# Graph attention over sorted edges: the reverse scan of maxima in halves, its marks in PSUM, q's products in two banks

## The chip, the cores and the metric

The kernel runs on one core of a Trainium2 chip. The metric is the device time of one execution in microseconds (us); the median of several runs counts. The engines are PE (TensorE), DVE (VectorE), ACT (ScalarE), POOL (GpSimd) and SP (SyncE, which here issues DMAs). PE writes its results to PSUM, eight banks of 512 fp32 columns for each of the 128 partitions; everything else lies in SBUF or in HBM. POOL has no access to PSUM in this kernel and does nothing in the stage of interest but issue gathers (indirect DMAs) and write zeros.

## The reference

A graph network layer on 6250 nodes of 128 features and 200,000 edges sorted by their target `dst`: two convolutions over the edges, then an attention of 8 heads with 16 columns each. The change touches the attention alone:

```python
q = (h @ qw + qb).reshape(n, H, HD)
k = (h @ kw + kb).reshape(n, H, HD)
v = (h @ vw + vb).reshape(n, H, HD)
logits = (q[dst] * k[src]).sum(-1) * scale + (edge_attr @ ew + eb)
amax = jax.ops.segment_max(logits, dst, num_segments=n)
pe = jnp.exp(logits - amax[dst])
ssum = jax.ops.segment_sum(pe, dst, num_segments=n)
w = pe / jnp.clip(ssum[dst], 1e-06)
o = jax.ops.segment_sum(w[:, :, None] * v[src], dst, num_segments=n)
```

All of it is fp32.

## The kernel before

The edges are cut into 196 chunks of 1024 (`CH`), each of eight tiles of 128 (`NT`). Since `dst` is sorted, a chunk's targets lie in a window of 112 nodes, so q of the targets is fetched by a product with a one-hot matrix, and sums over targets are products with another one. k and v of the sources are fetched from HBM by gathers: eight per chunk, each 128 rows of 256 fp32 numbers, issued by POOL at L621, followed by four memsets (L633) as a pause. A gathered chunk `g` has one of eleven buffers (L1155), which is free again when the chunk's `v` has been made (L1236).

The attention works in runs: eight chunks make a run, and the last three runs have six, four and two. `pipeline` (L712) is a loop over iterations n; in iteration n it

- starts loads and gathers of chunk n+1 (`fetch`), and prepares its one-hot `ohT` on ACT (`compared`, L614 and L615, in place);
- calls `second`: if a run ended with chunk n-1, its maxima are made (`maxima`, L1197), in pieces between other work; and one chunk of the run before, some nine chunks back, is finished: the comparison `oh` (L638), the addition of the chunk before it to the tables (L1262 to L1268), the weighted values `v` (ACT at L1235, L1337 and L1338, DVE at L1236), the sums `u` on PE (L1243), and the merging of the chunk before (L1250 to L1258, L1276, L1279);
- calls `first` for chunk n: `logits` (L1174) multiplies the gathered k by q (L1179, in three pieces of three, three and two tiles), copies the edges' bias out of PSUM (ACT, L1180), reduces by heads (L1182) and adds (L1184);
- moves a batch of finished nodes one step on (`attention_nodes`, L863; a batch of four windows starts every eight iterations from iteration 44 on, and uses DVE at L867 to L895 and L786 to L788);
- makes q's products of chunk n+1 on PE (`products`, L1163): `ohT` times the rows `pk`, eight tiles into three PSUM tiles `qe` of one bank each (L1166, three buffers), so that they are ready one iteration ahead.

DVE, ACT, PE and SP each keep the order in which the program issues (`in_order`, L700); POOL's gathers follow their buffers. fp32 products take two passes on PE per tile of 128 edges: 16 passes for a chunk's `u`, 16 for its `qe`.

`maxima` gives every edge the maximum of its segment within the run, for up to 64 rows (8 chunks times 8 heads) of 1024 edges. The logits are transposed in two halves of 512 (`lt`, PSUM, L1208); a forward scan over each half (L1211) takes the running maximum, and adds -1e30 where a segment begins (marks `nbs`). One reverse scan over all 1024 (L1214) then carries each segment's last value back, with the marks `nbe` of where segments end. Both marks are bf16 in SBUF, `fw` is fp32 in SBUF. Eight transposes (L1218) bring the result back as `rm`; L1222 subtracts it from the logits, ACT takes the exponential `pe` (L1224), and L1226 picks the maxima at the segments' ends (`wl`).

In PSUM the stage has `iota`, three banks of `qe`, `blk` (shared by `lt`, `rm` and the nodes' products), `pe` and two of `u`: all eight banks.

Of the kernel before, what the change touches and what calls it, by code (L numbers as in the profile page):

```python
# [8 lines left out]
FP = mybir.dt.float32  # L9
# [3 lines left out]
ALU = mybir.AluOpType  # L13
# [8 lines left out]
P = 128  # L22
D = 128
H = 8
HD = 16
NT = 8
CH = NT * P
REST = 4
G = 8
# [5 lines left out]
KW = WN + KE  # L35
DB = D + H
# [4 lines left out]
BIG = 1e30  # L41
# [4 lines left out]
def kernel(ctx: ExitStack, tc: tile.TileContext, x, src, dst, eat, w, out):  # L46
# [9 lines left out]
    nc = tc.nc  # L56
    N = x.shape[0]
    EW = src.shape[1]
    NCH = EW // NT
# [74 lines left out]
    a_d = {i: dram.tile([(NW + 1) * P, D], FP, name=f"a_d{i}") for i in (1, 2, 3)}  # L134
# [549 lines left out]
    def left_rows(k, pools, rows_d, tag, shape, bufs):  # L684

        lp = pools["left"]
        k.rows = lp.tile([P, DB], FP, name="l_rows")
        nc.vector.memset(k.rows[:, D:], 0.0)
        nc.sync.dma_start(out=k.rows[:, :D], in_=rows_d[bass.ds(k.win * P, P), :])
        onehot(k, pools, iota_j)  # L690
        k.ohf = lp.tile([P, NT, P], FP, name="l_ohf")
        per = shape[1]
        for a in range(0, NT, per):
            n = min(per, NT - a)
            tp = pools["ps"].tile(shape, FP, name="l_tp", tag=tag, bufs=bufs)
            for t in range(n):
                nc.tensor.transpose(tp[:, t, :P], k.oh[:, a + t, :], ident)
            nc.scalar.copy(k.ohf[:, a:a + n, :], tp[:, :n, :P])
# [453 lines left out]
    with ExitStack() as es:  # L1152
        pool = lambda n, b, **kw: es.enter_context(tc.tile_pool(name=f"{n}a", bufs=b, **kw))
        pools = {"oh": pool("oh", 2), "ps": pool("ps", 1, space=PSUM)}
        gp, wk, vp = pool("gp", G + 3), pool("wk", 2), pool("vp", 1)  # L1155
        ps_ = pools["ps"]
# [4 lines left out]
        TB = 3  # L1161

        def products(k, terms):  # L1163

            for a in range(0, NT, TB):
                qe = ps_.tile([P, TB, DB], FP, name="qe", tag="qe", bufs=3)  # L1166
                for t in range(min(TB, NT - a)):
                    e = slice((a + t) * P, (a + t + 1) * P)
                    for j, (lhs, rhs) in enumerate(terms):
                        nc.tensor.matmul(qe[:, t, :], lhsT=lhs[:, e], rhs=rhs,  # L1170
                                         start=(j == 0), stop=(j == len(terms) - 1))
                k.qe.append(qe)

        def logits(k, lg):  # L1174
            ebs = wk.tile([P, NT, H], FP, name="ebs")
            for a, qe in zip(range(0, NT, TB), k.qe):
                n = min(TB, NT - a)
                kk = k.g[:, a:a + n, :D]
                nc.vector.tensor_tensor(kk, qe[:, :n, :D], kk, ALU.mult)  # L1179
                nc.scalar.copy(ebs[:, a:a + n, :], qe[:, :n, D:])  # L1180
            l3 = wk.tile([P, NT, H], FP, name="l3")
            nc.vector.tensor_reduce(  # L1182
                l3, k.g[:, :, :D].rearrange("p t (h c) -> p t h c", c=HD), AX.X, ALU.add)
            nc.vector.tensor_tensor(lg, l3, ebs, ALU.add)  # L1184
# [12 lines left out]
        def maxima(run, lg, nb, bp):  # L1197

            n, c0 = len(run), run[0].c
            q = n * H
            fw = bp.tile([G * H, CH], FP, name="fw")
            half = CH // 2
            for a in range(2):
                lt = ps_.tile([G * H, 4, P], FP, name="lt", tag="blk")
                for t in range(4):
                    nc.tensor.transpose(lt[:q, t, :], lg[:, 4 * a + t, :n, :].rearrange("p c h -> p (c h)"), ident)  # L1208
                yield
                at = slice(a * half, (a + 1) * half)  # L1210
                nc.vector.tensor_tensor_scan(  # L1211
                    fw[:q, at], nb["nbs"][:q, at], lt[:q].rearrange("p t e -> p (t e)"),
                    fw[:q, half - 1:half] if a else -BIG, ALU.add, ALU.max)
            nc.vector.tensor_tensor_scan(  # L1214
                fw[:q, ::-1], nb["nbe"][:q, ::-1], fw[:q, ::-1], -BIG, ALU.add, ALU.max)
            rm = ps_.tile([P, NT, G, H], FP, name="rm", tag="blk")
            for t in range(NT):
                nc.tensor.transpose(rm[:, t, :n, :].rearrange("p c h -> p (c h)"), fw[:q, t * P:(t + 1) * P], ident[:q, :q])  # L1218
            yield
            wl = vp.tile([P, NT, G, H], FP, name="wl")  # L1220
            e3 = ef[:, c0 * NT:(c0 + n) * NT].rearrange("p (c t) -> p t c", t=NT)
            nc.vector.tensor_tensor(lg[:, :, :n, :], lg[:, :, :n, :], rm[:, :, :n, :], ALU.subtract)  # L1222
            pe = ps_.tile([P, NT, G, H], FP, name="pe", tag="pe")
            nc.scalar.activation(pe[:, :, :n, :], lg[:, :, :n, :], AF.Exp)  # L1224
            for t in range(NT):
                nc.vector.tensor_tensor(  # L1226
                    wl[:, t, :n, :], rm[:, t, :n, :], e3[:, t, :, None].to_broadcast([P, n, H]), ALU.mult)
            for j, k in enumerate(run):
                k.pe, k.wl = pe[:, :, j, :], wl[:, :, j, :]
# [56 lines left out]

        class Stage:
            sums, late, nb = [], [], None
            lg, j = None, 0

            def __init__(self, bp):
                self.bp = bp
# [8 lines left out]
                return k  # L1301

            def products(self, k):
                products(k, [(k.ohT[:KW], k.pk[:KW])])

            def first(self, k):
                if self.j == 0:
# [2 lines left out]
                self.j += 1  # L1310

            def reduce(self, k):
                pass

            def root(self, run):
                if self.nb is None and self.runs:
# [2 lines left out]
            def second(self, run, ks):  # L1319


                pieces = iter(())
                if run:
                    pieces = maxima(run, self.lg, self.nb, self.bp)
                    self.nb, self.j = None, 0
                for n, k in enumerate(ks):
                    mine = pieces if n == len(ks) - 1 else iter(())
                    next(mine, None)
                    onehot(k, pools, iota)
                    next(mine, None)  # L1330


                    if self.late:
                        add_late(self.late.pop(0))
                    next(mine, None)
                    weighted(k)
                    nc.scalar.copy(k.v[:, :, VK:VK + H], k.wl)  # L1337
                    nc.scalar.copy(k.v[:, :, VK + H], ef[:, k.c * NT:(k.c + 1) * NT])  # L1338
                    sums(k, VK + H + 1)
                    if self.sums:  # L1340
                        merge_late(self.sums[0])
                        self.late.append(self.sums.pop())
                    self.sums.append(k)
                for _ in pieces:
                    pass

            def batch(self, j):
                w = nc.values_load(at_i[3][0:1, j:j + 1], engines=[DVE, SP], min_val=0,
# [15 lines left out]

        def left(k):
            lp = pools["left"]
            left_rows(k, pools, a_d[3], "qe", [P, TB, DB], 3)
            k.g = gp.tile([P, NT, KV], FP, name="g")
            gather(k, k.g, kv_d, pause=False)
            k.qe = []  # L1370
            products(k, [(k.ohf.rearrange("p t e -> p (t e)"), k.rows), (k.ea, webl)])
            lg = lp.tile([P, NT, H], FP, name="l_lg")
            logits(k, lg)
            neg = lp.tile([P, 4, P], FP, name="l_neg")
            part = lp.tile([P, H, 2], FP, name="l_part")
            junk = lp.tile([P, 4, P], FP, name="l_junk")
            for a in range(2):
                nc.vector.tensor_scalar(neg, k.ohf[:, 4 * a:4 * a + 4, :], 1.0, BIG, ALU.subtract, ALU.mult)
                for h in range(H):
                    bc = ps_.tile([P, 4, P], FP, name="l_bc", tag="blk")  # L1380
                    for t in range(4):
                        nc.tensor.transpose(bc[:, t, :], lg[:, 4 * a + t, h:h + 1].to_broadcast([P, P]), ident)
                    nc.vector.tensor_tensor_reduce(
                        junk, bc, neg, 1.0, -BIG, ALU.add, ALU.max, part[:, h, a:a + 1])
            cm = lp.tile([P, H], FP, name="l_cm")
            nc.vector.tensor_reduce(cm, part, AX.X, ALU.max)
            me = ps_.tile([P, NT, H], FP, name="l_me", tag="pe")
            for t in range(NT):
                nc.tensor.matmul(me[:, t, :], lhsT=k.ohf[:, t, :], rhs=cm, start=True, stop=True)
            nc.vector.tensor_tensor(lg, lg, me, ALU.subtract)  # L1390

            nc.vector.tensor_scalar(lg, lg, 0.0, None, ALU.min)
            k.pe = lp.tile([P, NT, H], FP, name="l_pe")
            nc.scalar.activation(k.pe, lg, AF.Exp)
            weighted(k)
            sums(k, VK)
            tt = t3[:, bass.ds(k.win, 1), :]
            merge(k, M[:, bass.ds(k.win, 1), :], None, cm[:, None, :], 1)
            add(k, tt, 1)
# [43 lines left out]
```

## Time and profile before

| what | us |
|---|---|
| median of 3 runs | 7322.78 (7318.51 to 7324.84) |
| profiled execution | 7334.91 |
| its span | 7333.2 |
| first gather of the attention starts | 4865.6 |
| last one ends | 7255.3 |

| 4860 to 7260 us | busy us of 2400 | instructions |
|---|---|---|
| POOL | 1876.05 | 2352 |
| DVE | 1693.49 | 3755 |
| PE | 1322.40 | 6815 |
| PE weight loads | 1230.38 | 6813 |
| ACT | 732.95 | 2045 |

The DMA engines were busy 51% of this stretch, at 139 GB/s, and PE's granted clock was 0.72 of full speed.

How to read the profile's lines: a group has its source line, engine and operation, what it writes and reads (`out<-in`), the shape, the count, then the busy time in us and the mean duration in ns, then how long the engine was idle just before these instructions and what ended that. "issue" is idle time that ended with nothing the profile shows. A line of the waits has the waiting instruction, what ended the wait, and the total in us, the number and the longest. A line of the timeline has the start and the duration in us; neighbours of the same kind are merged, with their count. A reader should keep in mind that an engine's share of busy time does not tell whether it sets the pace; who waits for whom does.

### The profile page before, as it was taken

The page shows a single profiled execution, that of the slowest core. Times are in us where ns is not written, and L with a number is a line of the kernel's source. Part 1 is how long each engine was busy: PE and PEld are TensorE (multiplying, and loading weights), DVE is VectorE, ACT ScalarE, POOL GpSimd, SP SyncE. Part 2 cuts the span into 40 slices and gives each one's busy share as a digit, 9 for nine tenths or more (in the row PEclk, how much of TensorE's full clock was granted, in tenths as well). Part 3 has the DMA queues.
Part 4 walks back from the last instruction along what each step waited for, and adds up shares of the span by engine and source line. Part 5 has one row for each costly group of instructions (what it writes and reads, how often), then busy time and mean ns, then how long its engine had stood idle before and what let it go on. Part 6 is the DMA issues. An engine that isn't in the chain of part 4 may idle for free. (4 is left out here: it accounts for less than half of the span.)

```text
span 7333.2 us, 74261 instructions
## 1 busy us (share of the span) xinstructions
PE 3791.1 (52%) x20957; PEld 3613.5 (49%) x20958; DVE 5146.2 (70%) x7564; ACT 3312.2 (45%) x5293; POOL 5573.4 (76%) x7070
## 2 busy tenths in 40 slices
PE   4445454445554454455455555545555555555554
PEld 4444444445544444454454554444545555555554
DVE  6766677677777566666777777746667777777777
ACT  5555555555555455555555555532223333333332
POOL 6777777777777577777777777767777777777774
PEclk7777777777777667767777777767777777777777
DMA  5433333333333333333333333345445555555553
GB/s 144 108 94 92 85 106 89 97 94 94 98 96 92 77 88 89 91 90 87 97 99 101 97 100 103 99 102 137 135 135 142 141 138 145 143 142 138 140 139 86
DMA packets 414323, 800.46 MB, mean 109 GB/s; under 512 B 101813, under 2 KB 274984, under 8 KB 379496
## 3 DMA queue, kind: packets, MB, share of 16 engines
q0 software_dynamic: 175616, 411.34, 21.5%
q1 hardware_dynamic: 232646, 380.69, 19.1%
q10 hardware_dynamic: 5632, 3.51, 0.2%
q8 instruction: 172, 2.82, 0.2%
q14 instruction: 257, 2.11, 0.1%
HBM read 754.19 MB, written 40.96 MB: 108 GB/s over the span
## 5 line engine op out<-in xcount | busy, mean ns | idle before, releaser
L621 POOL DMA_INDIRECT g<-b_d,src_i x3136 | 3004.4, 958 | 979.9 <-issue 958.0
L1023 PE MATMUL u<-h,oh 128*128 128x129 f32 (+1 forms) x6272 | 1352.3, 402 | 2290.3 <-ACT h L1018 1952.6
L1023 PEld LDWEIGHTS u<-h,oh 128*128 128x128 f32 x6272 | 1248.2, 304 | 2365.9 <-ACT h L1018 2005.9
L621 POOL DMA_INDIRECT g<-kv_d,src_i x1568 | 1539.8, 982 | 502.1 <-issue 471.7
L999 DVE TENSOR_TENSOR h<-m,g 128x1024 f32<-128x1024 f32 x392 | 479.3, 1223 | 1055.6 <-DMA g<-b_d,src_i 939.4
L1243 PE MATMUL u<-v,oh 128*128 128x145 f32 x3136 | 754.0, 427 | 767.2 <-DVE nm L1276 553.2
L1243 PEld LDWEIGHTS u<-v,oh 128*128 128x128 f32 x3136 | 702.0, 310 | 801.9 <-issue 801.9
L633 POOL MEMSET nst<- 128x392 f32 x2352 | 1011.3, 430 | 101.7
L993 PE MATMUL m<-pk,ohT 117*128 117x128 f32 x6272 | 926.7, 311 | 29.1 <-ACT ohT L615 24.9
L993 PEld LDWEIGHTS m<-pk,ohT 117*128 117x128 f32 x6272 | 917.0, 232 | 30.9 <-ACT ohT L615 25.2
L1018 ACT ACTIVATE h<-h 128x1024 f32<-128x1024 f32 x392 | 414.1, 1056 | 1118.2 <-DVE h L1017 693.3
L1001 ACT ACTIVATE sq<-h 128x1024 f32<-128x1024 f32 x392 | 414.0, 1056 | 933.7 <-DVE h L999 657.8
L1002 DVE TENSOR_REDUCE var<-sq 128x64 f32<-128x1024 f32 x392 | 477.7, 1219 | 296.7 <-ACT sq L1001 240.2
L1179 DVE TENSOR_TENSOR g<-qe,g 128x384 f32<-128x384 f32 (+1 forms) x588 | 294.1, 511 | 554.4 <-DMA g<-kv_d,src_i 450.0
L614 ACT ACTIVATE ohT<-ohT,minus_p 112x1024 f32<-112x1024 f32 x588 | 670.3, 1140 | 14.9 <-DMA ohT<-rel_d 14.6
L615 ACT ACTIVATE ohT<-ohT 112x1024 f32<-112x1024 f32 x588 | 621.2, 1057 | 18.6
L1170 PE MATMUL qe<-pk,ohT 117*128 117x136 f32 x3136 | 515.8, 320 | 158.0 <-ACT ebs L1180 106.5
L1170 PEld LDWEIGHTS qe<-pk,ohT 117*128 117x128 f32 x3136 | 477.7, 226 | 192.1 <-ACT ebs L1180 130.8
L1016 DVE TENSOR_TENSOR h<-h,cps 128x1024 f32<-128x1024 f32 x392 | 478.4, 1220 | 13.5
L1017 DVE TENSOR_TENSOR h<-h,cps 128x1024 f32<-128x1024 f32 x392 | 478.4, 1220 | 13.4
L1013 DVE TENSOR_TENSOR h<-h,cps 128x1024 f32<-128x1024 f32 x392 | 475.3, 1213 | 5.9
L638 DVE TENSOR_TENSOR oh<-cps,dm 128x1024 f32<-128x1024 f32 x392 | 476.0, 1214 | 0.0
(265 smaller groups left out, 4380.3 us busy)
## 6 DMA issues: line engine op xcount, KB each, us to landing
ohT<-rel_d SPq DMA_DIRECT2D x294, 896.0 KB
g<-b_d,src_i POOLq DMA_INDIRECT x3136
pk<-a_d SPq DMA_DIRECT2D x588, 56.0 KB
g<-kv_d,src_i POOLq DMA_INDIRECT x1568
ohT<-in_eat_dram SPq DMA_DIRECT2D x294, 40.0 KB
a_d<-n_o SPq DMA_DIRECT2D x28, 256.0 KB
kv_d<-n_o SPq DMA_DIRECT2D x28, 256.0 KB
n_h<-h_d SPq DMA_DIRECT2D x19, 256.0 KB
```

Of the source, the lines that this page charges most:

```text
L614: nc.scalar.activation(k.ohT[:WN, :], k.ohT[:WN, :], AF.Square, bias=minus_p[:WN])
L615: nc.scalar.activation(k.ohT[:WN, :], k.ohT[:WN, :], AF.Relu, bias=1.0, scale=-4.0)
L621: return nc.gpsimd.indirect_dma_start(out=g[:, t, :table_d.shape[1]], out_offset=None, in_=table_d, in_offset=bass.IndirectOffsetOnAxis(ap ...
L633: last = nc.gpsimd.memset(nst2, 0.0)
L993: nc.tensor.matmul(k.m[:, t, :], lhsT=lhs[:, t * P:(t + 1) * P], rhs=rhs, start=(j == 0), stop=(j == len(terms) - 1))
L999: nc.vector.tensor_tensor(k.mt, k.m, k.g, ALU.add)
L1002: return lambda: nc.vector.tensor_reduce(var[:, j * NT * H:(j + 1) * NT * H], sq.rearrange("p t (g c) -> p (t g) c", c=HD), AX.X, ALU.add)
L1016: nc.vector.tensor_tensor(k.mt, k.mt, over_edges(gam), ALU.mult)
L1017: nc.vector.tensor_tensor(k.mt, k.mt, over_edges(bet), ALU.add)
L1023: nc.tensor.matmul(k.u[:, :wide], lhsT=k.oh[:, t, :], rhs=k.h[:, t, :wide], start=(t == 0), stop=(t == NT - 1))
L1170: nc.tensor.matmul(qe[:, t, :], lhsT=lhs[:, e], rhs=rhs, start=(j == 0), stop=(j == len(terms) - 1))
L1243: nc.tensor.matmul(k.u[:, :wide], lhsT=k.oh[:, t, :], rhs=k.v[:, t, :wide], start=(t == 0), stop=(t == NT - 1))
```

## The change

Three things are changed, all in the attention:

1. The reverse scan is made in two halves of 512, the later half first, and the earlier half starts from the first value of the later one. The marks of the segments' ends are copied beforehand from SBUF to a PSUM tile `ends` (fp32, one bank, one buffer) by ACT, half by half; the second copy is issued after the first half scan, whose tile it takes over.
2. `qe` has two banks in place of three, which makes the bank for `ends` free. A chunk's third piece of q's products (two tiles) is issued within `logits`, after the first piece has been multiplied and copied out; the first two pieces are issued one iteration ahead as before.
3. The order of the last parts of `maxima` moves: after the first half of the reverse scan comes the weighting, summing and merging of an earlier chunk; the second half and the transposes `rm` come after that; and L1222 to L1226 (subtraction, exponential, maxima at the ends) come after `first`, in `reduce`, except at the very end of the edges.

The path for chunks whose edges do not fit a window (`left`) follows the same form.

```diff
         def products(k, terms):
             for a in range(0, NT, TB):
-                qe = ps_.tile([P, TB, DB], FP, name="qe", tag="qe", bufs=3)
+                if a == 2 * TB:
+                    yield
+                qe = ps_.tile([P, TB, DB], FP, name="qe", tag="qe", bufs=2)
...
         def logits(k, lg):
             ebs = wk.tile([P, NT, H], FP, name="ebs")
-            for a, qe in zip(range(0, NT, TB), k.qe):
+            for a in range(0, NT, TB):
+                qe = k.qe[a // TB]
                 n = min(TB, NT - a)
                 kk = k.g[:, a:a + n, :D]
                 nc.vector.tensor_tensor(kk, qe[:, :n, :D], kk, ALU.mult)
                 nc.scalar.copy(ebs[:, a:a + n, :], qe[:, :n, D:])
+                if a == 0:
+                    next(k.rest, None)
...
+            def ends_of(a):
+                t = ps_.tile([G * H, half], FP, name="ends", tag="ends")
+                nc.scalar.copy(t[:q], nb["nbe"][:q, a * half:(a + 1) * half])
+                return t
+
+            ends = ends_of(1)
             for a in range(2):
                 lt = ps_.tile([G * H, 4, P], FP, name="lt", tag="blk")
...
-            nc.vector.tensor_tensor_scan(
-                fw[:q, ::-1], nb["nbe"][:q, ::-1], fw[:q, ::-1], -BIG, ALU.add, ALU.max)
+            for a in (1, 0):
+                at = slice(a * half, (a + 1) * half)
+                nc.vector.tensor_tensor_scan(
+                    fw[:q, at][:, ::-1], ends[:q, ::-1], fw[:q, at][:, ::-1],
+                    -BIG if a else fw[:q, half:half + 1], ALU.add, ALU.max)
+                if a:
+                    ends = ends_of(0)
+                    yield
             rm = ps_.tile([P, NT, G, H], FP, name="rm", tag="blk")
...
         class Stage:
-            lg, j = None, 0
+            lg, j, pieces = None, 0, iter(())
...
             def products(self, k):
-                products(k, [(k.ohT[:KW], k.pk[:KW])])
+                k.rest = products(k, [(k.ohT[:KW], k.pk[:KW])])
+                next(k.rest)
...
             def reduce(self, k):
-                pass
+                for _ in self.pieces:
+                    pass
...
-                for _ in pieces:
-                    pass
+                next(pieces, None)
+                self.pieces = pieces
+                if not ks or run and run[-1].c == NCH - 1:
+                    self.reduce(None)
```

## The prediction

> **What bounds the kernel now.** I read the page first, then the attention stage alone (its first gather starts at 4865.6 us, its last ends at 7255.3 us), because the whole change lies there. The groups by line and shape of 5200 to 7200 us:
>
> ```profile
> L621 POOL DMA_INDIRECT g<-kv_d,src_i x1309 | 1287.6, 984 | 404.6 <-issue 395.8 <-DVE wl L1226 5.4 <-DVE g L1179 2.7
> L1243 PE MATMUL u<-v,oh 128*128 128x145 f32 x2636 | 639.1, 429 | 665.8 <-DVE nm L1276 460.8 <-issue 150.5 <-DVE v L1236 53.9
> ...
> L633 POOL MEMSET nst<- 128x392 f32 x656 | 282.0, 430 | 28.4
> ...
> L1214 DVE TENSOR_TENSOR_SCAN fw<-nbe,fw 64x1024 f32<-64x1024 bf16 x20 | 45.6, 2282 | 0.7
> ```
>
> POOL's rows fill the 2000 us (1287.6 + 404.6 + 282.0 + 28.4 = 2002.6), and its idle time is a constant 0.30 us between gathers: it waits for no buffer. POOL sets the pace: eight gathers 1.25 us from start to start (0.95 + 0.30) and 1.9 us of memsets are 11.9 us a chunk, 95.3 us a run of eight. The runs are really 97.86 us apart. The timeline around a reverse scan shows where most of the difference is:
>
> ```profile
> 6038.30 1.26 DVE L1211 TENSOR_TENSOR_SCAN fw<-nbs,fw,lt 64x512 f32<-64x512 bf16 x1
> 6038.60 0.95 POOL L621 DMA_INDIRECT g<-kv_d,src_i  x1 [0.30 <-issue]
> 6039.60 2.28 DVE L1214 TENSOR_TENSOR_SCAN fw<-nbe,fw 64x1024 f32<-64x1024 bf16 x1
> 6039.86 2.78 POOL L621 DMA_INDIRECT g<-kv_d,src_i  x1 [0.30 <-issue]
> ```
>
> The gather beside the reverse scan took 2.78 us in place of 0.95, and ended 0.76 us after the scan. The forward scan, with one SBUF and one PSUM input, left its neighbour at 0.95. Followed through all 26 reverse scans, 24 have such a gather (1.15 to 2.01 us too long, 40.8 us together, 1.83 in the median run); one lies over POOL's memsets, one after the last gather.
>
> DVE is second. Its waits between 5450 and 7150 us:
>
> ```profile
> DVE g L1179 <- DMA g<-kv_d,src_i: 271.3, 187, 4.6
> DVE g L1179 <- issue: 37.7, 39, 3.0
> ...
> DVE g L1179 <- PE qe L1170: 21.4, 13, 2.0
> DVE g L1179 <- PE u L1243: 11.7, 9, 2.0
> ```
>
> That is 342 us in 17.4 runs, 19.7 us a run: all the room DVE has before it, not POOL, sets the pace. Where DVE already runs without a wait for gathers, at the end of the stage, one chunk looks so:
>
> ```profile
> 7231.28 1.21 DVE L638 TENSOR_TENSOR oh<-iota,dm 128x1024 f32<-128x1024 f32 x1
> ...
> 7233.92 1.22 DVE L1236 TENSOR_TENSOR v<-g,pe 128x1024 f32<-128x1024 f32 x1
> ...
> 7235.28 3.60 PE L1243 MATMUL u<-v,oh 128*128 128x145 f32 x16 [4.37 <-DVE nm L1276]
> ...
> 7236.34 1.35 DVE L1179 TENSOR_TENSOR g<-qe,g 128x384 f32<-128x384 f32 x3
> ...
> 7237.73 1.22 DVE L1182 TENSOR_REDUCE l<-g 128x64 f32<-128x1024 f32 x1
> ...
> 7238.71 2.02 PE L1170 MATMUL qe<-pk,ohT 117*128 117x136 f32 x16
> ...
> 7239.19 1.22 DVE L638 TENSOR_TENSOR oh<-iota,dm 128x1024 f32<-128x1024 f32 x1
> ```
>
> From comparison to comparison it is 7.91 us. The three products with q (L1179) run back to back while PE is still in u's 16 passes: q's products were made one chunk earlier.
>
> **The change, part by part.**
>
> *Reverse scan in halves, marks in PSUM.* Each half then has one SBUF and one PSUM input, like the forward halves, beside which no gather is long. POOL gains up to 40.8 us; a run on POOL falls to 97.86 - 1.83 = 96.0 us. Bounds: nothing, if the reverse form still stops POOL; 51.8 us, the whole excess of the 1568 gathers over 0.949 us. I take 40.8, since the forward row is nearly the same instruction. DVE pays two halves of about 1.25 us (the second forward half) for 2.28: +0.2 a run.
>
> The Trainium skill (SBUF — State Buffer, "Who interferes with whom") speaks against this gain: it has a two-SBUF-input DVE instruction contend only with a GpSimd instruction that reads SBUF, and infers that making DMA descriptors is not stopped by one, as it needs the write interface. The 2.78 us row contradicts that for these gathers; by the rule POOL's 40.8 us would be nothing, by the row they are real.
>
> *The copies.* 52 ScalarE copies of 512 columns, about 0.60 us each (the Exp at L1224, 512 columns into PSUM: 0.601), are 31 us on an engine busy 733 of 2400 us. The first of a run stands ahead of the scans, behind nothing urgent. The second waits for the first reverse half, and queued behind it is L1235, for which DVE's L1236 waits: half scan, copy, L1235 and hand-overs are 1.2 + 0.6 + 0.27 + 0.1 = 2.15 us before L1236, as the old scan's 2.2 was. Net nothing.
>
> *The rest of the maxima behind the next chunk's products.* The transposes rm (8 passes, 1.05 us) now follow the second half and stand on PE between u and the third piece: +1.05 a run on the path below. The second half (1.25) lies inside DVE's new wait.
>
> *The third piece.* This is the part that decides. On PE the third piece of chunk n now comes after u of the same iteration, and DVE's third product waits for it. Counted from the start of L1236: u starts at +1.36 (7235.28 - 7233.92), lasts 3.87 us (639.1 us / 164.75 groups of 16), then four passes of about 0.14 us, 0.6 with the last one's tail (16 take 2.02), and 0.1 of hand-over: ready at +5.93. DVE wants it at +3.36 (7236.34 plus two products of 0.47). When DVE is not waiting for gathers, each chunk so costs it 2.57 us more: 7.91 becomes 10.48. As long as DVE waits for gathers anyway the wait is covered; that cover is the 19.7 us.
>
> The sum for a run, in DVE's chain: 8 x 10.48 = 83.8; the run's end 1.13 + 1.30 (forward halves, start to start) + 2.15 + 1.05 + 1.65 (L1222 and eight L1226) = 7.3; the node batch's eight 512-column operations of 0.68 to 0.70 and three small ones, 6.4. Before, the same sum is 8 x 7.91 + 6.3 + 6.4 = 76.0, with 19.7 of waits 95.7, and 97.86 was measured: 2.2 us a run are unlisted, and I keep them. After: 83.8 + 7.3 + 6.4 + 2.2 = **99.7 us** a run. That is over POOL's new 96.0, and over the old 97.86. Runs without a node batch (the first five) need 93.3 and stay on POOL.
>
> u's length is the large unknown, and the timeline bounds it:
>
> ```profile
> 7267.73 2.22 PE L1243 MATMUL u<-v,oh 128*128 128x145 f32 x16 [1.77 <-DVE nm L1276]
> ...
> 7276.90 4.21 PE L1243 MATMUL u<-v,oh 128*128 128x145 f32 x16 [6.95 <-DVE nm L1276]
> ```
>
> 2.22 us after 1.77 us of idle PE, 4.21 after 6.95. At 2.22 the wait is 0.92 and a run 86.5, so POOL decides; at 4.21 the wait is 2.9 and a run 102.4. I take the stage's mean, 3.87, because PE's idle time in the new chunk (10.48 less 3.87, 0.6 and 1.5 for two pieces: 4.5 us) is like that before most groups now.
>
> The Trainium skill (TensorE: Matmul & The Clock Gate, "What's actually happening") has PE go to half clock after about 3.4 us idle and back only after about 3.4 us busy. By that rule 4.5 us idle would make nearly every u a 4.2 us one, and the sum below would be 7412; by the row's mean it is 7364.
>
> *Hidden.* q's two banks: pieces 0 and 1 of the next chunk wait for pieces 1 and 2 of this one, and PE has iterations to spare. SP: the ohT load waits for the third piece, now one chunk (some 10 us) later; the loads are now issued 21 to 25 us before ScalarE's L614 uses them, and their packets take 4 to 5 us. The marks' and pk's loads queue behind it on SP and move with it, still before the products. If that cover were gone, L614 and the products would be late by the difference, up to some us a run.
>
> **The whole.** Against the profiled span of 7333.2 us: the first five runs save their stalls, -7; from the first node batch (about 5400) to DVE's last wait for a gather (7173) are 18.1 runs, 18.1 x (99.7 - 97.86) = +33; after 7173 DVE is alone the path, and the last seven chunks' third products wait for u (2.8, 1.1, 0.6, 1.0, 2.3, 1.9, 1.0 us, from the end of u plus 0.7 against each product's start), 10.7, and rm is uncovered in the last three runs, about 4: +15. Sum +41. The median of the runs, 7322.78, lies 10 us under the profiled span; the change is added to it: **7364 us**.
>
> **Rivals.**
> 1. *Faster: POOL keeps the pace.* If a run of DVE's chain stays under 96.0, all the stalls' 40.8 us come home, less the tail's 15: 7298. For it: POOL waits for nothing now, and a gather's buffer has been free for 11 us or more when it starts (end of L1236 of the chunk eleven before, against the gather's start). Against: 99.7. It decides below 2.1 us of wait a chunk, u below 3.4 us.
> 2. *Much slower: u always at half clock*, 102.4 a run: -7 + 18.1 x 4.5 + 15 = +90, 7412. For it: 4.5 us idle in each chunk; against: the mean of 3.87 under similar gaps.
> 3. *No change:* a run between 97 and 98.6 us leaves the total within 15 us of 7323.
> 4. *The reverse halves still stop POOL.* DVE's chain decides all the same, and only the first five runs lose their gain: 7371. The forward rows speak against it.
>
> **How the numbers follow.** My forecast (7338 to 7395) has 0.46, rival 1 0.20, rival 2 0.17, rival 3 0.13, rival 4 0.04. A difference under 0.2% (15 us) can't be told from none here. Slower: 0.46 + 0.17 + 0.04 = 0.67; same 0.13; faster 0.20. Both signs are in it, so the range goes from rival 1 to a little past rival 2: 7298 to 7418; the forecast's own is 7338 to 7395.
>
> **What would show it.** Right: no gather over 1.5 us beside a scan; DVE's L1179 waiting for PE's q products by some 15 to 20 us a run, its waits for gathers nearly gone; POOL's gathers, in later runs, waiting for DVE's L1236; runs about 99 to 100 us apart. Wrong: runs 96 us apart with POOL still idle only 0.30 us between gathers (rival 1), or long gathers that remain (rival 4). A mean u far from 3.9 us moves the total by some 145 us per us of it.

## The result, and the profile after

The changed kernel takes **7364.14 us** (median of 4 runs, 7362.51 to 7366.83), against 7320.65 us for the kernel before (4 runs, 7316.2 to 7324.84): a ratio of 1.0060, 95% interval 1.0042 to 1.0077. It is slower by 43.5 us. The profiled execution of after has a span of 7365.1 us, 31.9 us more than that of before, whose profiled execution (7334.91 us) lay some 14 us above its kernel's median.

The groups by line and shape of after, 5200 to 7200 us:

```profile
L621 POOL DMA_INDIRECT g<-kv_d,src_i x1308 | 1249.6, 955 | 444.1 <-issue 367.8 <-DVE cm L1299 60.1 <-DVE M L1274 8.4
L1263 PE MATMUL u<-v,oh 128*128 128x145 f32 x2616 | 655.8, 441 | 784.7 <-DVE nm L1296 784.7
...
L1183 DVE TENSOR_TENSOR g<-qe,g 128x256 f32<-128x256 f32 x161 | 68.4, 425 | 401.2 <-PE qe L1173 386.4 <-DMA g<-kv_d,src_i 14.9
...
L1230 DVE TENSOR_TENSOR_SCAN fw<-ends,fw 64x512 f32<-64x512 f32 x40 | 49.7, 1242 | 2.1
...
L1214 ACT CAST ends<-nbe 64x512 f32<-64x512 bf16 x40 | 23.1, 578 | 64.0 <-DVE fw L1230 64.0
```

The mean gather fell from 984 to 955 ns: the long ones are gone. (Summed over all 1568, the excess over 0.949 us went from 51.8 to 7.6 us, and no gather that overlaps a scan takes more than 0.96 us.) But POOL's waits now end with DVE's L1299, which runs just after `v` at L1256: it waits for a buffer. The third product with q, the one of 256 columns, waits 386.4 us for PE. The waits of DVE, 5450 to 7150 us, and of POOL in the same stretch:

```profile
DVE g L1183 <- PE qe L1173: 356.3, 137, 3.3
DVE mn L1270 <- DVE cm L1299: 48.2, 138, 0.7
DVE v L1256 <- ACT v L1255: 15.4, 18, 0.9
...
DVE g L1183 <- DMA g<-kv_d,src_i: 0.6, 2, 0.3
```

```profile
POOL g L621 <- issue: 306.7, 998, 2.1
POOL g L621 <- DVE cm L1299: 60.1, 62, 2.7
```

DVE's waits for gathers (271.3 us before) have gone to nothing, and every chunk's third product waits for PE: 356.3 / 137 = 2.60 us. DVE, with PE's u in its chain, now sets the pace and POOL follows. The timeline around a run's end shows both parts of the change at once:

```profile
6035.61 1.22 DVE L1230 TENSOR_TENSOR_SCAN fw<-ends,fw 64x512 f32<-64x512 f32 x1
6035.73 0.95 POOL L621 DMA_INDIRECT g<-kv_d,src_i  x1 [0.30 <-issue]
...
6036.86 0.58 ACT L1214 CAST ends<-nbe 64x512 f32<-64x512 bf16 x1 [3.00 <-DVE fw L1230]
6037.39 0.26 ACT L1255 COPY v<-pe 128x64 f32<-128x64 f32 x1
...
6037.68 1.22 DVE L1256 TENSOR_TENSOR v<-g,pe 128x1024 f32<-128x1024 f32 x1 [0.85 <-ACT v L1255]
...
6039.05 4.21 PE L1263 MATMUL u<-v,oh 128*128 128x145 f32 x16 [5.52 <-DVE nm L1296]
...
6040.02 1.27 DVE L1230 TENSOR_TENSOR_SCAN fw<-ends,fw 64x512 f32<-64x512 f32 x1
...
6043.19 1.08 PE L1238 MATMUL rm<-ident,fw 64*128 64x64 f32 x8
...
6044.20 2.41 PE L1173 MATMUL qe<-pk,ohT 117*128 117x136 f32 x16
...
6044.97 0.42 DVE L1183 TENSOR_TENSOR g<-qe,g 128x256 f32<-128x256 f32 x1 [2.77 <-PE qe L1173]
```

The gather beside the reverse half takes 0.95 us. u runs 4.21 us, rm stands behind it, then q's third piece, and DVE stands idle for 2.77 us until its first passes are there. Three `v` of the same run, on DVE:

```profile
6100.47 1.21 DVE L1256 TENSOR_TENSOR v<-g,pe 128x1024 f32<-128x1024 f32 x1
6110.92 1.21 DVE L1256 TENSOR_TENSOR v<-g,pe 128x1024 f32<-128x1024 f32 x1
...
6136.67 1.22 DVE L1256 TENSOR_TENSOR v<-g,pe 128x1024 f32<-128x1024 f32 x1 [0.85 <-ACT v L1255]
```

A chunk with no node work is 10.45 us long here, and from 6037.68 to 6136.67 a run is 98.99 us. The length of a run is given below as the mean between the `v` of chunk 48 and that of chunk 176, sixteen runs: 97.89 us before, 98.99 after. Where the time went, in us from each kernel's first attention gather (which starts 2.8 us earlier in after):

| | before | after | difference |
|---|---|---|---|
| `v` of chunk 48 is made | 698.2 | 695.2 | -3.0 |
| `v` of chunk 176 is made | 2264.5 | 2279.0 | +14.5 |
| POOL's last gather ends | 2389.7 | 2384.6 | -5.1 |
| end of the program | 2467.5 | 2502.2 | +34.7 |

POOL ends earlier and the program later. Eleven buffers let POOL run ahead of DVE, and the lag that DVE builds up is paid after the last gather: 117.6 us from there to the end, 77.9 before. (POOL's buffers were last read at least 11.4 us before they were filled again in before, and as little as 0.3 us in after.)

### The profile page after: what moved, and what is told of

Read it like the earlier page. It is cut to its first block, busy times and chain, and to the rows that moved or that the text cites. A ratio compares the mean times of both kernels' runs of the same rounds, so it can differ in the third digit from the quotient of the medians.

```text
span 7365.1 us, 74292 instructions
## 1 busy us (share of the span) xinstructions
PE 3687.7 (50%) x20957; PEld 3510.2 (48%) x20958; DVE 5134.9 (70%) x7590; ACT 3330.8 (45%) x5345; POOL 5524.1 (75%) x7070
## 5 line engine op out<-in xcount | busy, mean ns | idle before, releaser
L1023 PE MATMUL u<-h,oh 128*128 128x129 f32 (+1 forms) x6272 | 1290.1, 389 | 2407.0 <-ACT h L1018 2407.0
L1023 PEld LDWEIGHTS u<-h,oh 128*128 128x128 f32 x6272 | 1189.1, 292 | 2482.8 <-ACT h L1018 2474.3
L621 POOL DMA_INDIRECT g<-kv_d,src_i x1568 | 1495.6, 954 | 542.0 <-issue 443.6
L1263 PE MATMUL u<-v,oh 128*128 128x145 f32 x3136 | 777.7, 437 | 907.2 <-DVE nm L1296 905.5
L1263 PEld LDWEIGHTS u<-v,oh 128*128 128x128 f32 x3136 | 726.8, 320 | 944.9 <-issue 944.9
L993 PE MATMUL m<-pk,ohT 117*128 117x128 f32 x6272 | 884.1, 301 | 29.4 <-ACT ohT L615 28.2
L993 PEld LDWEIGHTS m<-pk,ohT 117*128 117x128 f32 x6272 | 870.1, 222 | 31.0 <-ACT ohT L615 29.1
L1173 PE MATMUL qe<-pk,ohT 117*128 117x136 f32 x3136 | 532.3, 322 | 142.7 <-ACT ebs L1184 73.8
```

The lines of the kernel that those rows point to most:

```text
L621: return nc.gpsimd.indirect_dma_start(out=g[:, t, :table_d.shape[1]], out_offset=None, in_=table_d, in_offset=bass.IndirectOffsetOnAxis(ap ...
L993: nc.tensor.matmul(k.m[:, t, :], lhsT=lhs[:, t * P:(t + 1) * P], rhs=rhs, start=(j == 0), stop=(j == len(terms) - 1))
L1023: nc.tensor.matmul(k.u[:, :wide], lhsT=k.oh[:, t, :], rhs=k.h[:, t, :wide], start=(t == 0), stop=(t == NT - 1))
L1173: nc.tensor.matmul(qe[:, t, :], lhsT=lhs[:, e], rhs=rhs, start=(j == 0), stop=(j == len(terms) - 1))
L1263: nc.tensor.matmul(k.u[:, :wide], lhsT=k.oh[:, t, :], rhs=k.v[:, t, :wide], start=(t == 0), stop=(t == NT - 1))
```

## The experiments

The theory: the halves with marks in PSUM free POOL; the late third piece makes DVE's chain longer than POOL's, by u's length, and takes the gain and more. The rivals: the marks' place doesn't matter; the loss lies in the halves and copies; POOL still sets the pace. Each kernel ran beside the kernel before on the same chip; its median there was 7319.63 us for e1 to e4, 7320.47 for e5 to e8, 7321.83 for e9 and e10.

**e1: the marks stay in SBUF**, the rest of the change as it is.

```
-            ends = ends_of(1)
...
-                    fw[:q, at][:, ::-1], ends[:q, ::-1], fw[:q, at][:, ::-1],
+                    fw[:q, at][:, ::-1], nb["nbe"][:q, at][:, ::-1], fw[:q, at][:, ::-1],
...
-                    ends = ends_of(0)
```

> The changed kernel with one part undone: the reverse halves read their marks from SBUF again, and the copies to PSUM are gone. If two SBUF inputs are what stops POOL, the gathers beside the halves grow long again (about 1 us each, two a run). If DVE's chain sets the pace, that costs nearly nothing in all: POOL waits some 3 us a run for buffers in the changed kernel, which swallows it; only the first runs, without node batches, lose up to 2 us each, and the wait of DVE's L1256 for the copy (0.85 us a run) goes: 7350 to 7375 us. Rival, POOL sets the pace: 40 us more, about 7404. Rival, the port is not the matter: no long gathers.

Measured: 7351.96 us, ratio 1.0043 (1.0029 to 1.0057). The long gathers are back, beside the halves (timeline of e1):

```profile
6128.63 1.22 DVE L1224 TENSOR_TENSOR_SCAN fw<-nbe,fw 64x512 f32<-64x512 bf16 x1
6128.87 1.73 POOL L621 DMA_INDIRECT g<-kv_d,src_i  x1 [0.30 <-issue]
...
6132.31 1.27 DVE L1224 TENSOR_TENSOR_SCAN fw<-nbe,fw 64x512 f32<-64x512 bf16 x1
6132.79 1.55 POOL L621 DMA_INDIRECT g<-kv_d,src_i  x1 [0.30 <-issue]
```

Each ends 0.75 us after its half, as the gather of before ended 0.76 us after the whole scan. So do 30 of the 37 gathers that start within a half, eleven of them over 0.5 us too long; the other seven, all begun within 0.08 us of the half's start, keep their 0.95 us. In after all 37 do. So the marks' move to PSUM does free POOL. It is worth nothing here, since a run stays 99.0 us and POOL only waits less for its buffers than the 60.1 us of after:

```profile
POOL g L621 <- DVE cm L1292: 37.7, 44, 2.6
```

The median is 12.2 us under after's, and every run of e1 lies under every run of after. The traces show only 3.5 us of this in the attention, 2498.7 against 2502.2 us from the first gather to the end; 6.0 us lie ahead of it (the first gather starts at 4856.8 us in e1 and at 4862.9 in after), where the two kernels have the same code. e1 also leaves out the copies of the marks, so the 3.5 us may be theirs.

**e2: the scan's part alone**, on the kernel before, with its three banks for q; the copied marks go to the bank `blk`, which the logits' transposes have just left. The order of the maxima stays that of before.

```
+            for a in (1, 0):
+                at = slice(a * half, (a + 1) * half)
+                ends = ps_.tile([G * H, half], FP, name="ends", tag="blk")
+                nc.scalar.copy(ends[:q], nb["nbe"][:q, at])
...
-                fw[:q, ::-1], nb["nbe"][:q, ::-1], fw[:q, ::-1], -BIG, ALU.add, ALU.max)
```

> The kernel before with the scan's part of the change alone: halves, marks copied to PSUM, but into the bank that the logits' transposes have just left, so that q's products keep three banks and stay one chunk ahead. My theory: the stalls go, the third product waits for nothing, runs are 96 us apart, 7321 - 41 + 5 for DVE's two waits for copies in the last runs = 7285 us (7275 to 7295). Rival, the halves, the copies or the order around them are what costs time: 7321 or more.

Measured: 7283.75 us, ratio 0.9953 (0.9936 to 0.9969); a run is 95.8 us, and no gather beside a scan is long. DVE still waits for gathers, POOL for nothing (waits of each, 5450 to 7150 us):

```profile
DVE g L1179 <- DMA g<-kv_d,src_i: 259.6, 197, 4.7
```

```profile
POOL g L621 <- issue: 339.2, 1101, 2.1
```

The gain is 35.9 us in the medians and 43.9 in the attention alone (2423.6 us from the first gather to the end, 2467.5 before). POOL's gathers together fell from 1539.8 to 1491.4 us, 48.4 less, and the time after the last one grew from 77.9 to 83.1.

**e3: the late third piece alone**, two banks, on the kernel before (the diff's changes to `products`, `logits` and `Stage.products`, nothing of the scan).

> The kernel before with the other part alone: two banks for q's products and the third piece late; the reverse scan as it was. My theory: the third product waits about 2.6 us where DVE is not waiting for gathers; a run's chain is 99.0 less the 1.05 us of the transposes, 98.0, against POOL's 97.86 with its stalls: both nearly alike, so little in the middle and 11 us at the end, 7330 to 7350 us. Rival, the third piece is hidden: 7321.

Measured: 7335.76 us, ratio 1.0023 (1.0013 to 1.0033). Waits of DVE in e3:

```profile
DVE g L1183 <- PE qe L1173: 186.9, 98, 3.1
DVE g L1183 <- DMA g<-kv_d,src_i: 163.8, 129, 3.2
```

The two waits share one gap: DVE still waits for gathers in most chunks, so POOL with its long gathers (23 of the 24 that start within a scan) still sets the pace (a run is 97.9 us), and the loss (16.1 us in the medians, 8.6 in the attention) is in the end, 91.5 us after the last gather in place of 77.9. By the medians the parts are worth -35.9 and +16.1 alone, -19.8 by addition, and +43.5 together; by the attention's length in the traces -43.9, +8.6 and +34.7. The 63 or 70 us between sum and whole are the finding: the scan's part only gains while POOL sets the pace, and the piece's part only loses fully once POOL doesn't. Neither e2 nor e3 has the third part of the change, the new order of the maxima, so this difference holds its cost too, and no run has it alone; e4, which has it, shows that it doesn't bring DVE's chain over POOL's by itself.

**e4: the third piece ahead of u.** The changed kernel, with the last u of an iteration issued on PE after the third piece.

```
                 if a == 0:
                     next(k.rest, None)
+                    if then:
+                        then()
...
-                    sums(k, VK + H + 1)
+                    if n < len(ks) - 1:
+                        sums(k, VK + H + 1)
+                    else:
+                        self.owed = k
```

> The changed kernel with one order altered: u's 16 passes are issued behind the third piece of q's products, not ahead of it. u is not needed before the next iteration's merge. My theory: the third product's wait falls from 2.6 us to about 0.6, POOL sets the pace again without the stalls, 96 us a run: 7280 to 7300 us. Rival, u late takes its place (merge or the next v wait for it): 7330 and more. Rival, the order on PE is not the cause: 7364.

Measured: 7304.5 us, ratio 0.9976 (0.9966 to 0.9986). Timeline of e4, then its DVE waits:

```profile
6090.32 1.27 PE L1173 MATMUL qe<-pk,ohT 117*128 117x136 f32 x4 [4.84 <-ACT ebs L1184]
...
6091.39 4.07 PE L1265 MATMUL u<-v,oh 128*128 128x145 f32 x16
6091.64 0.42 DVE L1183 TENSOR_TENSOR g<-qe,g 128x256 f32<-128x256 f32 x1 [1.11 <-PE qe L1173]
```

```profile
DVE g L1183 <- DMA g<-kv_d,src_i: 128.3, 52, 8.1
DVE g L1183 <- PE qe L1173: 122.5, 110, 1.6
DVE v L1258 <- ACT v L1257: 53.8, 34, 3.0
```

With u out of the third piece's way its wait falls to 1.1 us (122.5 / 110), POOL sets the pace again (96.0 us a run, waiting for no buffer), and 59.6 us of the changed kernel's 7364 go, with the same halves and copies. That settles where the loss is. It missed its range by 4.5 us: u is now late, the copy into `v`'s one buffer waits for it (ACT 50 times, 36.2 us, and DVE in turn, last line), and the end after the last gather is 100.5 us, 17.4 more than in e2.

**e5: the third piece's passes twice**, to double the suspected cost.

```
-                for t in range(min(TB, NT - a)):
+                for t in 2 * list(range(min(TB, NT - a))) if a == 2 * TB else range(TB):
```

> The changed kernel with the third piece's products made twice (same result, four more passes of about 0.13 us in each chunk). If DVE's chain runs through this piece, each chunk costs 0.5 us more, a run 4.0 to 4.5, 18 runs and the end 76 to 85: 7425 to 7460 us. Rival, PE has room there: 7364.

Measured: 7433.72 us, ratio 1.0158 (1.0141 to 1.0175), a run is 102.4 us. Four more passes a chunk in front of DVE's third product cost 3.4 us a run (0.43 a chunk), and 69.6 us in all: DVE's chain runs through this piece.

**e6: PE kept busy.** The changed kernel with 24 passes a chunk whose result nobody reads, issued after the first two pieces, into the marks' bank.

```
                 next(k.rest)
+                warm = ps_.tile([G * H, CH // 2], FP, name="warm", tag="ends")
+                for _ in range(12):
+                    nc.tensor.matmul(warm[:, :DB], lhsT=k.ohT[:KW, :G * H], rhs=k.pk[:KW],
+                                     start=True, stop=True)
```

> The changed kernel with 24 passes of products without a reader behind the first two pieces of the next chunk, in PE's idle stretch, written to the bank of the marks. They are ahead of nothing that is waited for. If PE's clock stays up by them, u takes about 2.2 to 2.6 us in place of 3.97, the third product's wait falls to about 1 us, a run's chain to about 88, and POOL sets the pace at 96: 7280 to 7305 us, with more work done. If the clock does not stay up: 7364. Rival, the third product's wait is not what costs time: u short and 7364.

Measured: 7317.07 us, ratio 0.9999 (0.9989 to 1.0009). Groups of e6, 5200 to 7200 us:

```profile
L1328 PE MATMUL warm<-pk,ohT 117*64 117x136 f32 x3983 | 530.3, 293 | 0.0
L1263 PE MATMUL u<-v,oh 128*128 128x145 f32 x2704 | 472.6, 339 | 379.5 <-DVE nm L1296 379.5
```

530 us of useless work on PE made the kernel 47 us faster than the changed one. u's 16 passes fell from 4.01 us (655.8 / 163.5 groups) to 2.80 (472.6 / 169), the granted clock of the run rose from 0.736 to 0.785, the third product's wait fell to 1.82 us (216.6 / 119), and a run is 96.0 us. The clock records of the traces, laid over each u of these 2000 us, show why u is shorter: where the granted clock was 1.0 all through, u takes 2.22 to 2.26 us, where it was 0.5 all through, 4.20 to 4.21. Of after's 164 u, 2 are of the first kind and 78 of the second; of e6's 169, 107 and 19. The others lie between. So the size of the loss is set by PE's clock during u. It came out 12 us above its range: the end is 110.9 us, and PE waits longer for `pk`'s loads (85.7 us in these 2000, 39.2 in after).

**e7 to e10: POOL's pause.** If POOL doesn't set the pace in the changed kernel, two memsets after a chunk's gathers in place of four (in the attention alone) should gain little; in e2, where it does, much.

```
-                for _ in range(REST):
+                for _ in range(REST if table_d.shape[1] == D else REST // 2):
```

e7, on the changed kernel:

> The changed kernel with two memsets in POOL's pause in place of four, in the attention alone: POOL needs 0.95 us less a chunk, 7.6 a run. If DVE's chain sets the pace at 99.0 us a run, only the first five runs gain, from 95.1 to about 92.6: 7340 to 7358 us. Rival, POOL sets it: 196 x 0.95 = 186 us less, about 7180.

e8, on e2:

> The scan's part alone (three banks for q's products) with POOL's pause halved in the attention. If POOL sets the pace there, each run loses 7.6 us: about 7285 - 23 x 7.6 = 7110 us (7095 to 7160). If DVE's chain or the gathers' landing takes over first, less is gained; DVE's own chain there is 76.0 + 2.2 + 1.7 = 80 us a run, so it should not.

Measured: e7 7337.15 us, ratio 1.0024 (1.0015 to 1.0034); e8 **7109.34 us**, ratio 0.9716 (0.9700 to 0.9732), the fastest kernel of the study. In e7 the `v` of chunk 48 is made 27.3 us sooner than in after, counted from the first gather, and from there to the end both take 1807.0 us: the first runs gain all of it, 3 us more than the range allowed, and a run stays 99.0. POOL spends the rest waiting for buffers (5450 to 7150 us):

```profile
POOL g L621 <- DVE cm L1299: 217.5, 101, 3.7
```

In e8, within its range, a run is 88.3 us. Two more kernels asked how much of that is the pause alone. e9, the halved pause on the kernel before:

> The kernel before with POOL's pause halved in the attention and nothing else, to tell what of the 7109 us of the scan's part with the halved pause belongs to the pause. If POOL sets the pace in the kernel before, a run falls from 97.86 by 7.6 to 90.2 us: 7320 - 23 x 7.6 = 7145 us (7130 to 7165), and the scan's part is worth its 37 us there too. Rival, the pause holds something else back: 7200 and more.

e10, e2 with no pause in the attention at all:

> The scan's part alone, and no pause of POOL in the attention. POOL's floor is then eight gathers of 1.25 us, 80.2 a run, and DVE's chain, 76.0 + 2.2 + 1.7 = 80, has no room left. Were both as fast as that: 7109 - 23 x 7.6 = 6935 us. With two engines at their limit, waits for gathers and for buffers come in: 6950 to 7060 us.

Both expectations failed badly, and only e9's rival had the direction: e9 7619.03 us, ratio 1.0402 (1.0384 to 1.0419), e10 7869.34 us, ratio 1.0743 (1.0725 to 1.0761). Waits of POOL and DVE in e9, 5450 to 7150 us:

```profile
POOL g L621 <- DVE cm L1279: 318.6, 61, 9.5
```

```profile
DVE v L1236 <- ACT v L1235: 254.4, 46, 10.0
DVE g L1179 <- remote: 79.1, 49, 4.1
DVE g L1179 <- PE qe L1170: 53.4, 22, 3.8
```

POOL, with less to do, waits longer, and DVE waits up to 10 us for ACT's copy at a place where it hardly waited before (0.7 us in all); a run is 108.2 us. The scan's stalls are not what e9 pays: no gather overlaps a scan in it, and none is over 0.5 us too long. The DMA engines are busy 46% of that stretch and move 128 GB/s, against 58% and 155 in e8 (5450 to 7000 us). ACT's copy waits in its turn, and what for the trace doesn't name (183.8 us put down to "remote", a signal for which it found no instruction of this core). By these two runs the pause holds off something that costs more than it does; the first sign of it, waits of 8.6 to 15.5 us at L1179, which reads gathered rows and q's products, stands in e9's first chunks (4908 to 4986 us). The cause stays open, and with it how much of e8's gain the scan's part may claim: e8 is good as measured, and near an edge.

## Why the prediction was right

**The direction and the mechanism.** The step "This is the part that decides" was right: the third product waits for u, DVE's chain becomes longer than POOL's, and POOL waits for buffers. e4 and e6 show it from both sides, by moving u away and by making it short; e5, which lengthens the third piece, and e7, which gives POOL less to do, agree. Its price was predicted as 2.57 us a chunk and measured as 2.60; the chunk as 10.48 and measured as 10.45 and 10.31 where no node work lies in it; u as 3.87 and measured as 4.01. With u 0.14 us over its estimate and the wait only 0.03 over, the wait's other terms were together a little too large.

**The stalls.** The 40.8 us taken for POOL's gain were too few (POOL's gathers lost 48.4 in e2, near the upper bound of 51.8), without weight here: once DVE decides, a run is 99.0 with part of the stalls back (e1) or with none. The prediction reads the 2.78 us row as contradicting the whole rule that it quotes from the Trainium skill. The gathers read `src_i`, an SBUF tile (L94), so a rule on GpSimd instructions that read SBUF covers them; what the row speaks against is the inference on making descriptors. Which of the two is held up, no run here tells.

**The threshold.** Rival 1 was to decide below a wait of 2.1 us a chunk. It did: with 1.1 us (e4) and 1.8 us (e6) runs are POOL's 96.0, with 2.6 us (after, e7) 99.0; the change lies somewhere between 1.8 and 2.6. Rival 2's condition, u always at half clock, held for 78 of the 164 u of after (5200 to 7200 us), and the mean of 4.01 us lies close to the half clock's 4.21. The rival priced a run at 102.4, for a wait of 2.9; at the measured 2.6 it is 99.0.

**The sum, term by term.** The total is right partly because errors cancel:

| term | predicted | measured |
|---|---|---|
| a run in DVE's chain | 99.7 us | 98.99 |
| the run before | 97.86 | 97.89 |
| first runs | -7 | -3.0 |
| runs on DVE's chain | 18.1 x 1.84 = +33 | 16 x 1.10 = +17.5 |
| the stage's end | +15 | +20.2 |
| the sum | +41 | +34.7 from the first gather, +31.9 in the spans, +43.5 in the medians |

The mis-sized term is the run: 99.7 is 0.7% over 98.99, but only its difference to 97.86 counts, and of that 1.84 us the 0.7 is 40%. The end was under-counted: from chunk 176 on before took 203.1 us and after 223.3. (The prediction's stages lie a little differently: it counted 18.1 runs, from about 5400 us on, the table 16.) The sum was made for the span, where it is 9 us too large; added to the median it hit the result to a microsecond, and that is luck as much as sizing. The 11.6 us between the spans' difference and the medians' come mostly from the profiled execution of before. Part of it can be seen: its first attention gather starts at 4865.6 us, the latest of the twelve profiled executions (4856.7 to 4865.6, all with the same code ahead); after's starts 2.8 us sooner. Where the other 9 lie stays open.

**The copies.** "2.15 us" from the first reverse half to L1256 was 2.07 (6035.61 to 6037.68). DVE stands still for 0.85 us of it, and yet "net nothing" held: without the copies a run is as long (e1), and the attention 3.5 us shorter.

**The loads.** "Still before the products" was wrong: between 5450 and 7150 us PE waited 14 times for `pk` (33.1 us, up to 4.5). It cost little: in the same stretch DVE's products waited 0.6 us for gathers and otherwise for the third piece alone, and e4, with the same order of loads, is POOL's.

## What to carry to other kernels

Before a resource is freed, work out the second-longest chain with the change in it: here POOL gained 2.1 us a run (97.89 to 95.8 in e2), and DVE's chain, 19.7 us below it, was lengthened by 8 x 2.60. Two edits that each leave the pace-setter in place can't be added; price them together, and test each alone. In a queue that runs in order, what is issued late waits for what is issued ahead of it, whatever its own length: here q's third piece, four passes, waited for u's 4.01 us.

## What the runs showed of the hardware

- An indirect gather that starts within a scan of two SBUF operands ends about 0.76 us after the scan, whether that is 2.28 us long (24 of 24 in before, 23 of 24 in e3) or 1.22 (30 of 37 in e1, the others begun within 0.08 us of the scan's start); with one operand in PSUM none was lengthened (after, e2).
- Passes whose result nobody reads, in PE's idle time, shorten the real ones: u from 4.01 to 2.80 us, and the kernel by 47 us (e6). In after and e6, u's 16 passes take 2.22 to 2.26 us at a granted clock of 1.0 and 4.20 to 4.21 at 0.5.
- A shorter pause between gathers can cost time: halved, the kernel before went from 7321.83 to 7619.03 us; taken out of e2, 7283.75 became 7869.34; halved in e2, it became 7109.34. What decides between the two was not found.
